# First layers of five blocks as seven products of half sums, second layers as one product at the end

## The chip, the cores and the metric

The kernel runs on one core of a Trainium2 chip. The metric is device time in microseconds (us): 341.78 us, the median of three runs (341.9, 341.78 and 339.52). The engines of the core are named as in the profile: PE (TensorE, matmul), DVE (VectorE), ACT (ScalarE), POOL (GpSimd) and SP (SyncE, which issues nearly all the DMAs here). They run side by side and wait for each other on semaphores.

## The reference

`x` is (2, 512, 1024), the context is (2, 1024, 1024). Both batches together are 1024 tokens of width 1024.

```python
def fake_quant(x, s, z):
    return (clip(round(x / s + z), 0, 255) - z) * s

x = x + tanh(g_xattn[0]) * matmul(fake_quant(layernorm(x)), fake_quant(ctx))

xt = layernorm(x).reshape(1024, 1024)
scores = softmax(xt @ router_w + router_b) + router_bias       # 16 experts
# 2 of 4 groups of experts, then 2 experts of those groups; gate = their scores
def step(y, p):
    w1, b1, w2, b2, w3, b3, ge = p
    h = silu(xt @ w1 + b1) * (xt @ w2 + b2)                    # 1024 -> 256
    return y + ge[:, None] * (h @ w3 + b3)                     # 256 -> 1024
y = scan(step, 0, all 16 experts)
z = silu(xt @ sw1 + sb1) * (xt @ sw2 + sb2) @ sw3 + sb3         # 1024 -> 512 -> 1024
x = x + tanh(g_ffn[0]) * (y + z)
```

With the inputs at hand all tokens choose the same two experts, so that two of the sixteen do work.

## The kernel before

**Precision.** The quantised product is exact in bf16. Every other large product is made to fp32 accuracy by splitting each operand into a high and a low part (`hi` is the operand cast to fp32r by ACT, `lo` the rest, a subtraction on DVE), and by three matmul passes: high times high, high times low, low times high. `split` (L308) does both steps for one operand.

**Tiling.** The tokens are 8 tiles of 128 (`NT`), 4 in each of the two batches; the contraction of 1024 is 8 slices of 128 (`KD`). A first-layer *block* is 128 hidden columns of `w1` and `w2` for all tokens: 4 shared ones (`SC`) and 2 for each expert (`EC`). For one block and one batch, `up_mm` (L327) accumulates w1's and w2's results in two PSUM banks with 2 x 3 x 8 matmuls of 128x512 (L335), so that a block is 96 matmuls. `up_post` (L341) applies bias, SiLU and gate product (L345 on ACT, L346 on DVE) and splits the hidden layer into its two parts. The second layer (`down`, L374) takes 128 tokens and accumulates all blocks of the shared network, or of one expert, in two PSUM banks; DVE then adds it, times the gate, onto the residual `X[t]` in SBUF (L386). A tile of the shared network takes 24 matmuls, one of an expert 12. Biases of the second layer are added by DVE from a broadcast row (`add_bias`, L393).

**Order.** The first part, up to 94.7 us, is a list written out by hand (`START`, L50, run under `manual_schedule`): layernorm, quantisation, attention product, second layernorm, transposes into `XH` and `XL` (the split activations with the contraction on partitions), and the first batch of shared columns 0 to 2 (steps `um`, `us`, `ug`, with `uh` and `ul` splitting the hidden). A step name is followed by its arguments: `mm.3.5` is the attention product of tile 3, slice 5. After this list the order is that of the code, and a planner puts it onto the engines' queues: shared column 0 for batch 1 (two halves), the router's input of batch 0 (`router_x`, L558: POOL adds `XH` and `XL` in four pieces, L563), shared column 1, the router's product (`router_logits`, L570), column 2, the router's product of batch 1, column 3 for both batches with the expert selection between (`choose` L607, a chain of small DVE operations, `count` L641 with one matmul, `next_expert` L652 twice, whose index is read into a register of SP at L673). Then `shared_down` (L704) for all 8 tiles, expert 0 (two blocks, then 8 tiles of second layer), expert 1. Weights come by SP's queue: `load_up` (L316) brings w1 and w2 of one block, 512 KB each; `load_down` (L353) a 128-row piece of `w3`. An expert's loads need its index.

**Buffers.** 22 `slabs` of 4 KB per partition hold raw and split weights and hidden parts in turn; `X` stays in SBUF for the whole run (8 tiles in `keep`), and so do `XH` and `XL`. A load into a slab waits until the slab's last user is through.

**End.** The last tile's second layer (`down_last`, L361) goes in columns of 512, 256 and 256. Two dynamic branches follow: one (L784, L785) repeats everything in a slower exact form if the quantisation's zero points don't fit; the other (L802 to L804) loops over further experts, if more than two were chosen. Neither is taken.

## Time and profile before

| | |
|---|---|
| median of the runs | 341.78 us |
| profiled execution | 340.19 us |
| its span in the trace | 338.5 us |
| first matmul after the hand-ordered list | 94.70 us |
| PE busy from there to 329.4 us | 234.69 of 234.70 us |
| one 128x512 matmul in an expert's first layer (43.52 us / 192) | 0.2267 us |
| last DVE operation ends | 329.9 us |
| DVE, 128x1024, two SBUF inputs (e0a0l, L312) | 1.22 us |
| ACT, cast of 128x1024 (e0a0h, L310) | 1.05 us |

The profiled execution's own time is 1.7 us longer than the span, and 1.6 us below the median of the runs. A row of the page's groups gives line, engine, operation, output and inputs with their sizes, how many there were, busy time in us and mean ns of one, and the idle time of the engine ahead of them with what ended it. Where the output of a whole block is meant, `e0p` stands for the first-layer banks of expert 0, `sp` for those of the shared network, `spo` and `e0po` for second-layer banks.

Four groups of the page, for their sizes and durations:

```profile
L241 PE MATMUL at<-cq,qT 128*128 128x512 bf16 x128 | 30.2, 379 | 2.4 <-POOL cq L161 1.4
L386 DVE SCALAR_TENSOR_TENSOR X<-spo,tg,X 128x512 f32<-128x512 f32 x16 | 11.3, 746 | 15.9 <-PE spo L383 15.9
L345 ACT ACTIVATE e0sa<-e0p,bv 128x512 f32<-128x512 f32 x4 | 2.8, 692 | 48.6 <-PE e0p L335 48.6
L394 DVE SCALAR_TENSOR_TENSOR X<-sbias,tg,X 128x1024 f32<-128x1024 f32 x8 | 10.3, 1285 | 0.3
```

DVE's and ACT's idle time in these rows is ended by PE: they have nothing to do until its matmuls are through.

### The profile page before, as it was taken

How to read it: one execution, taken by the hardware profiler on the slowest of the kernel's cores; microseconds unless marked ns; L12 is line 12 of the kernel's file. 1: busy time of each engine (PE TensorE's matmuls, PEld its weight loads, DVE VectorE, ACT ScalarE, POOL GpSimd, SP SyncE). 2: the span in 40 equal slices, each digit the busy share in tenths (PEclk: the TensorE clock that was granted, in tenths of full speed). 3: DMA queues.
4: the chain of work that ended last, by engine and by line, in shares of the span. 5: the costliest groups of instructions: out<-in, count | busy, mean ns of one | idle time of the engine just before them, and what ended most of it. 6: DMA issues, size and time to landing. Idle time of an engine off the chain costs nothing.

```text
span 338.5 us, 4322 instructions
## 1 busy us (share of the span) xinstructions
PE 318.1 (94%) x1673; PEld 254.7 (75%) x1673; DVE 197.0 (58%) x335; ACT 95.3 (28%) x148; POOL 78.6 (23%) x110
## 2 busy tenths in 40 slices
PE   6588899999999999999999999999999999999990
PEld 2244796769999776888888888888888888888870
DVE  3879999979812226845845441495385135944560
ACT  2657767873213135220200002211400012030000
POOL 2795798878600650000000000000000000000000
PEclk9799999999999999999999999999999999999996
DMA  6999940000004033100300092200410300001542
GB/s 190 420 375 381 409 106 0 2 0 2 0 2 124 3 126 124 64 0 25 99 2 0 0 293 81 63 2 12 112 62 2 124 0 2 0 0 61 191 185 75
DMA packets 25892, 31.45 MB, mean 93 GB/s; under 512 B 2492, under 2 KB 19204, under 8 KB 25860
## 3 DMA queue, kind: packets, MB, share of 16 engines
q1 hardware_dynamic: 25860, 31.05, 26.8%
q8 instruction: 17, 0.28, 0.3%
q14 instruction: 15, 0.12, 0.1%
HBM read 26.85 MB, written 4.19 MB: 92 GB/s over the span
## 4 chain that ended last, share of the span: by engine, by line
PE 75%; DVE 8%; POOL 5%; ACT 4%; issue 3%; DMA 2%; SPq 0%; DVEq 0%; POOLq 0%
PE sp L335 16%; PE e1p L335 13%; PE e0p L335 13%; PE sp L483 5%; PE spo L381 4%; PE spo L380 4%; PE spo L383 4%; ACT xn L262 2%; PE e0po L380 2%; PE e0po L383 2%; PE e0po L381 2%; PE e1po L380 2%; PE e1po L383 2%; PE e1po L381 2%; DMA X<-in_dram 2%
## 5 line engine op out<-in xcount | busy, mean ns | idle before, releaser
L241 PE MATMUL at<-cq,qT 128*128 128x512 bf16 x128 | 30.2, 379 | 2.4 <-POOL cq L161 1.4
L563 POOL TENSOR_TENSOR xf<-XH,XL 128x1024 f32<-128x1024 f32 x8 | 19.9, 2498 | 22.3 <-PE sp L335 19.5
L241 PEld LDWEIGHTS <-qT 128*128 128x128 bf16 x128 | 12.2, 98 | 15.4 <-issue 2.8
L386 DVE SCALAR_TENSOR_TENSOR X<-spo,tg,X 128x512 f32<-128x512 f32 x16 | 11.3, 746 | 15.9 <-PE spo L383 15.9
L346 DVE SCALAR_TENSOR_TENSOR ssa<-sp,bT,ssa 128x512 f32<-128x512 f32 (+1 forms) x6 | 4.0, 662 | 25.2 <-PE sp L335 25.2
L345 ACT ACTIVATE e0sa<-e0p,bv 128x512 f32<-128x512 f32 x4 | 2.8, 692 | 48.6 <-PE e0p L335 48.6
L386 DVE SCALAR_TENSOR_TENSOR X<-e0po,gv,X 128x512 f32<-128x512 f32 x16 | 11.3, 746 | 7.3 <-PE e0po L383 7.3
L386 DVE SCALAR_TENSOR_TENSOR X<-e1po,gv,X 128x512 f32<-128x512 f32 x14 | 9.9, 745 | 8.2 <-PE e1po L383 8.2
L291 DVE TENSOR_SCALAR xn<-X,nm,d 128x512 f32<-128x512 f32 x16 | 13.8, 890 | 1.0 <-POOL d L287 0.9
L345 ACT ACTIVATE e1sa<-e1p,bv 128x512 f32<-128x512 f32 x4 | 2.8, 689 | 34.1 <-PE e1p L335 34.1
L296 PE MATMUL px<-ident,xn 128*128 128x128 f32 x64 | 9.3, 275 | 3.0 <-DVE xn L291 1.9
L262 ACT ACTIVATE xn<-X,s 128x512 f32<-128x512 f32 x16 | 11.4, 716 | 1.9 <-DVE X L253 1.4
L173 DVE BATCH_NORM_STATS2 st<-X 128x6 f32<-128x512 f32 x16 | 10.3, 679 | 2.5 <-DMA X<-in_dram 2.5
L253 DVE SCALAR_TENSOR_TENSOR X<-at,cx_scale,X 128x512 f32<-128x512 f32 x16 | 11.6, 741 | 0.1
L346 DVE SCALAR_TENSOR_TENSOR e1sa<-e1p,bv,e1sa 128x512 f32<-128x512 f32 x4 | 3.0, 751 | 14.8 <-PE e1p L335 14.8
L296 PEld LDWEIGHTS px<-ident,xn 128*128 128x128 f32 x64 | 7.2, 141 | 5.0 <-ACT XH L153 2.2
L346 DVE SCALAR_TENSOR_TENSOR e0sa<-e0p,bv,e0sa 128x512 f32<-128x512 f32 x4 | 3.0, 750 | 13.5 <-PE e0p L335 13.5
L306 DVE TENSOR_TENSOR XL<-px,XH 128x512 fp32r<-128x512 f32 x16 | 10.4, 678 | 0.8 <-ACT XH L153 0.8
L394 DVE SCALAR_TENSOR_TENSOR X<-sbias,tg,X 128x1024 f32<-128x1024 f32 x8 | 10.3, 1285 | 0.3
L161 POOL TENSOR_SCALAR cq<-q8c,nz 128x1024 bf16<-128x1024 uint8 (+1 forms) x8 | 10.0, 1252 | 1.0 <-DVE q8c L231 0.6
L216 PE MATMUL pq<-ident_b,qx 128*128 128x128 bf16 x64 | 5.5, 231 | 4.6 <-ACT qx L159 4.3
L159 ACT ACTIVATE qx<-q8x,nz 128x1024 bf16<-128x1024 uint8 (+1 forms) x7 | 7.2, 1022 | 9.5 <-DVE q8x L205 9.5
(402 smaller groups left out, 830.0 us busy)
## 6 DMA issues: line engine op xcount, KB each, us to landing
cr<-in_dram SPq DMA_DIRECT2D x15, 512.0 KB, 9.9
out_dram<-X SPq DMA_DIRECT2D x15, 256.0 KB, 2.3
X<-in_dram SPq DMA_DIRECT2D x7, 512.0 KB, 9.2
X<-in_dram SPq DMA_DIRECT2D x2, 256.0 KB, 3.9
cr<-in_dram SPq DMA_DIRECT2D x2, 256.0 KB, 9.0
sb1r<-in_dram SPq DMA_DIRECT2D x1, 512.0 KB, 9.0
sa1r<-in_dram SPq DMA_DIRECT2D x1, 512.0 KB, 7.2
sb0r<-in_dram SPq DMA_DIRECT2D x1, 512.0 KB, 8.3
```

The costliest lines, as they stand in the source:

```text
L241: nc.tensor.matmul(acc[t][h], qT[b][:, t % TB, k, :], cq[b][:, k, half(h)], start=(k == 0), stop=(k == KD - 1))
L253: nc.vector.scalar_tensor_tensor(xs, acc[t][h], cx_scale, xs, ALU.mult, ALU.add, accum_out=sq_[t][0][:, h : h + 1])
L262: nc.scalar.activation(xn_[t][:, half(h)], X[t][:, half(h)], AF.Square, bias=s[:, h : h + 1], scale=-float(H), accum_out=q[:, h : h + 1],)
L291: nc.vector.tensor_scalar(xn_[t][:, half(h)], X[t][:, half(h)], nm, r, ALU.add, ALU.mult)
L296: nc.tensor.transpose(px_[t, q][:, k, :], xn_[t][:, ts(4 * q + k, P)], ident)
L335: nc.tensor.matmul(p, wx[:, k, :], xx[b][:, k, cols], start=first and k == 0, stop=last and k == KD - 1)
L380: nc.tensor.matmul(po[h], hh[:, ts(t, P)], wh[:, ts(h, 512)], start=first, stop=False)
L381: nc.tensor.matmul(po[h], hh[:, ts(t, P)], wl[:, ts(h, 512)], start=False, stop=False)
L383: nc.tensor.matmul(po[h], hl[:, ts(t, P)], wh[:, ts(h, 512)], start=False, stop=last)
L386: nc.vector.scalar_tensor_tensor(xs, po[h], scale, xs, ALU.mult, ALU.add)
L483: nc.tensor.matmul(up_[c, lo, i], w[:, k, :], x[0][:, k, lo : lo + 256], start=p == 0 and k == 0, stop=p == 2 and k == KD - 1,)
L563: nc.gpsimd.tensor_tensor(x, XH[b][:, ts(i, 2)].bitcast(F32), XL[b][:, ts(i, 2)].bitcast(F32), ALU.add)
```

## The change

Five blocks (shared column 3 and both blocks of both experts) no longer run as 96 matmuls but as seven products of 12. Tokens are halved by batch (index 1 and 2 of `A`), the contraction is halved (`KH` = 4 slices), and the two outputs, w1's and w2's, are the two column halves of `B`. This is Winograd's form of Strassen's scheme: sums S1 to S4 of activation halves are made once (from the router's unsplit inputs, in place), sums T1 to T4 of weight halves for every block, and the outputs are put together from seven products. All sums are split into high and low parts as other operands are.

Further: the hidden layer of every block and the residual pass through DRAM (`h_all`, `x_after`); the gate of an expert multiplies its hidden layer rather than its second layer's output, for which the gates of all tokens go to DRAM as one row and come back broadcast over the partitions; and the second layers of shared network and experts become one accumulation over all 8 blocks at the end, three tiles together first. The steps `uh` and `ul` leave the hand-ordered list, and `xd`, `ud`, `lv` (loads of w1 and w2 of shared column 2, taken out of `lw`) and `xx` come in. The pools become 16 slabs of 4 KB and 14 octs of 8 KB per partition, and `X` is in slabs. The two branches at the end become one.

```diff
-    slabs = ctx.enter_context(tc.tile_pool(name="slabs", bufs=22))
+    octs = ctx.enter_context(tc.tile_pool(name="octs", bufs=14))
+    slabs = ctx.enter_context(tc.tile_pool(name="slabs", bufs=NSLAB))
...
+    def xd(t):
+        nc.sync.dma_start(x_after[t], X[t])
+    def ud(c, lo):
+        nc.sync.dma_start(h_all[c][:, lo : lo + 256], sa_[c, lo])
...
+    def prep_pair(name, wa, wb):
...
+        split(wa, ah, al)
+        W["B11"], W["B21"] = (ah[:, lo], al[:, lo]), (ah[:, hi], al[:, hi])
...
+        sub = lambda out, p, q: nc.gpsimd.tensor_tensor(out, p, q, ALU.subtract)
+        sub(t13[:, lo], wb[:, lo], wa[:, lo])
+        sub(t24[:, lo], wb[:, hi], t13[:, lo])
+        sub(t13[:, hi], wb[:, hi], wb[:, lo])
+        sub(t24[:, hi], wa[:, hi], t24[:, lo])
+        for n, t in (("24", t24), ("13", t13)):
...
+            split(t, h, l)
...
+        W["B22"] = split(wb[:, hi], b22[:, lo], b22[:, hi])
+    def pair(name, W, b1, b2, ci, gates=None):
...
+        product(pa, "A11", "B11", True, False)
+        nc.scalar.copy(s1, pa)
+        product(pb, "S2", "T2", True, False)
+        nc.vector.scalar_tensor_tensor(s6, pb, b2, s1, ALU.add, ALU.add)
+        product(pa, "A12", "B21", False, True)
+        nc.scalar.activation(s11, pa, AF.Silu, bias=b1)
+        gated(s11, 0)
+        product(pb, "S3", "T3", False, False)
+        nc.vector.scalar_tensor_tensor(s7, pb, b2, s1, ALU.add, ALU.add)
+        product(pc, "S1", "T1", True, False)
+        product(pb, "A22", "T4", False, True)
+        nc.vector.tensor_tensor(s7, pc, s7, ALU.add)
+        nc.vector.tensor_tensor(s1, pb, s1, ALU.add)
+        nc.scalar.activation(s1, s1, AF.Silu, bias=b1)
+        gated(s1, 1)
+        product(pc, "S4", "B22", False, True)
+        done(s7, s1, 1)
+        nc.vector.tensor_tensor(s6, pc, s6, ALU.add)
+        done(s6, s11, 0)
...
+    wp = prep_pair("s3", *load_up("s", sw1c, sw2c, 3))
     sup(1, 1)
...
+    for i in range(2):
+        nc.vector.tensor_tensor(a22[i], a22[i], a21[i], ALU.add)
+    s1, s2, s3, s4 = a22, a11, a21, a12
+    for i in range(2):
+        nc.gpsimd.tensor_tensor(s3[i], a11[i], a21[i], ALU.subtract)
+    A["S2"] = sum_x("S2", s2, s1, a11, ALU.subtract, nc.vector)
+    for i in range(2):
+        nc.gpsimd.tensor_tensor(s4[i], a12[i], s2[i], ALU.subtract)
...
+    A["S3"] = split_x("S3", s3)
     sup(2, 1)
...
+    A["S1"] = split_x("S1", s1)
+    A["S4"] = split_x("S4", s4)
+    pair("s3", wp, sb1c(3), sb2c(3), 3)
...
+    for j, (e_, gv, bv) in enumerate(chosen):
+        nc.sync.dma_start(g_row[j].rearrange("(t p) -> p t", p=P), gv)
+        gates = slab(f"gates{j}", F32)
+        nc.sync.dma_start(gates, g_row[j].partition_broadcast(P))
+        for c in range(EC):
+            wp = prep_pair(f"e{j}_{c}", *load_up(f"e{j}", *expert_up(e_), c))
+            pair(f"e{j}_{c}", wp, bv[:, 0, c : c + 1], bv[:, 1, c : c + 1], SC + EC * j + c, gates)
...
+    for c in range(NC):
+        for n, src, got in (("h", h_all[c], hid), ("d", w3_rows(c), w3)):
+            raw = slab(f"{n}{c}r", F32)
+            nc.sync.dma_start(raw, src)
...
+    first, rest, last = (4, 5, 6), (7, 0, 1, 2), 3
...
-    zi = rt("zi", (P, 1), I32)
...
-    n_exp = nc.values_load(n_chosen[0:1, 0:1], min_val=2, max_val=E)
-    with tc.If(n_exp > 2):
-        with tc.For_i(2, n_exp):
-            expert(2, *next_expert(2), False)
```

The names that the prediction uses: in a block `x` (s3, e0_0, e0_1, e1_0, e1_1), `xs1`, `xs6` and `xs7` are the intermediate sums in SBUF, `t13` and `t24` the sums of weight halves (POOL, L378 of the changed kernel), `b22` the split lower half of w2; S3 and S4 are made on POOL at L739 and L742 of it. `done` stores the finished half of a hidden layer.

## The prediction

> **What bounds the kernel now.** I read four views. First the page's busy shares and its 40 slices:

> ```profile
> span 338.5 us, 4322 instructions
> PE 318.1 (94%) x1673; PEld 254.7 (75%) x1673; DVE 197.0 (58%) x335; ACT 95.3 (28%) x148; POOL 78.6 (23%) x110
> ...
> PE   6588899999999999999999999999999999999990
> ...
> PEclk9799999999999999999999999999999999999996
> ```

> From slice 11 on PE is full and at full clock, and POOL is idle after slice 15. Then the chain of waits in order of time:

> ```profile
> 94.86 22.43 PE sp L335 x144
> ...
> 198.76 43.52 PE e0p L335 x192
> 264.04 43.52 PE e1p L335 x192
> ```

> After the hand-ordered part the chain is PE alone. 43.52 us / 192 gives 0.2267 us for a 128x512 matmul. So a matmul removed there saves its full price, and any wait put in front of PE costs its full length, since nothing of PE is slack. Third, what feeds an expert. The timeline (start and length in us) of DVE's index and of SyncE's load issues:

> ```profile
> 157.26 0.14 DVE L657 TENSOR_SCALAR ei<-m 128x1 int32<-128x1 f32 x1
> ...
> 158.26 0.40 SPq L320 DMA_DIRECT2D e0a0r<-in_dram  x1
> 159.54 0.38 SPq L320 DMA_DIRECT2D e0b0r<-in_dram  x1
> ```

> Their landing (KB, us from issue) and the stretch up to expert 0's first matmul:

> ```profile
> e0a0r<-in_dram SPq DMA_DIRECT2D x1, 512.0 KB, 4.0
> e0b0r<-in_dram SPq DMA_DIRECT2D x1, 512.0 KB, 5.1
> ```

> ```profile
> 155.00:198.80 43.80, 43.80 (x196) 36.31 (x195) 26.06 (x49) 2.73 (x3) 0.00 (x0) 1.00 0.16 46
> ```

> Both weights of expert 0 had landed by 164.6 and PE took them up at 198.8. The last row (PE, PEld, DVE, ACT, POOL busy, clock, DMA share, GB/s) shows the shared second layer covering 34 us of loading and splitting. This cover is what the change removes. Fourth, rows that price POOL beside DVE: two of the timeline in the hand-ordered part and a group of the page (busy us, mean ns, idle before):

> ```profile
> 42.54 1.29 POOL L474 TENSOR_TENSOR sa0l<-sa0r,sa0h 128x512 fp32r<-128x512 f32 x1
> 42.60 1.24 DVE L190 TENSOR_TENSOR qa<-r,rs 128x1 f32<-128x1 f32 x1 [0.46 <-POOL r L186]
> L563 POOL TENSOR_TENSOR xf<-XH,XL 128x1024 f32<-128x1024 f32 x8 | 19.9, 2498 | 22.3 <-PE sp L335 19.5
> ```

> A DVE operation on one element per partition lasted 1.24 us, to the end of the POOL operation that had started just before it.

> [...] 4.29 us idle ahead of L216, and clock digit 7 in slice 2. [...] The change stores gate rows in 4-byte pieces; no row of before has such a store.

> **The change part by part**, against the profiled execution (340.2 us, of which the span is 338.5); the median of the runs, 341.8, is 1.6 higher. Prices without a line are the means of the same operation and size in before's groups: DVE 128x1024 with two SBUF inputs 1.22 (e0a0l), 128x512 0.68, a PSUM eviction 0.75; ACT's cast 1.05; POOL 128x512 1.28.

> *Matmuls.* Seven products of 12 matmuls take the place of 96: five blocks x 12 x 0.2267 = **-13.6 us**. Second layers keep 384 matmuls of 128x512 or their equal, so merging them saves PE nothing; 32 of 48 evictions (0.75 each) go, from a DVE that is 58% busy.

> *Hand-ordered part.* It loses the hidden splits (uh, ul) and gains stores of the residual and hidden on SP. The new waits: layernorm's buffer of tile 2 waits for the store of tile 0 (issued by about 40.5 here, needed at 53.8); the load of sa2r comes behind the store of tile 1 (lands about 49, needed 54.5). (Issue times are those of the same steps in before.) Both are hidden by attention's matmuls; if that cover is short, 2 us. I take **-0.5** (-2 to +2).

> *First Strassen block (shared column 3).* PE: both shared blocks and both router products are done by 120.8, sup(2,1) by 132.5, then the products at 2.72 each; the fourth (S3·T3) wants the second's bank evicted (s6) at 140.7. On DVE that eviction stands behind, all after the router's second product at 120.8 because the half sums overwrite the router's operands: 13 operations of 128x1024 (four sums, lo parts of t13, S1 to S4) at 1.22 = 15.9, b22 0.7, two evictions 1.5, some 20 small router operations 4.5. Total 22.6: 143.4, then 0.75 for itself, about 3 late. In the same stretch POOL does four 128x1024 subtractions for S3 and S4 at about 2.4. [...] 9.6 less what falls into DVE's waits, +7.5. s6 is then done near 151.3. Behind it: S3·T3 2.7, the s7 eviction 0.75, and the rest of the expert selection on DVE (some 20 x 0.22), on which PE's count matmul waits in the middle of the block; then A22·T4 and S4·B22, 5.4. The block ends near 162.5 instead of 151.5. I take **+10.5**; without lock +3, with twice its cost +14.

> *First expert block.* Before, the loads went out 1 us after the index. Now SP, in order, has ahead of them: the gate row's store (4-byte pieces), its broadcast reload that waits for it, and the two stores of the s3 hidden, the second of which waits for the last eviction of the s3 block. So the loads start after PE has run out of work, which is the change's largest wait: eviction and product 1.6, store issue and two loads 0.4 + 1.0 + 1.28 = 2.7 (the spacing of the rows above), landing 5.1, sharing with the gates' broadcast 1.0, four dependent POOL subtractions of 128x512 at 1.28 = 5.1, ACT's cast 1.05, handoffs 0.5. Together 17.1, less 2.7 for the first product, which needs only the w1 half: **+14.4** (13 to 18). The upper end is a slow gate row: the nearest row of before is the router weight's load in 64-byte pieces, 8.2 us beside other traffic; above some 4 us it holds the reload, and with it the expert's loads.

> *Second block of expert 0, then expert 1.* Within e0_0, 1.2. For e0_1: ACT's cast of the next block's t24 waits for four POOL subtractions on a late load and stands ahead of the PSUM copy e0_1s1, which the third product waits for: +4.5 (2.4 to 4.6). Sum **+5.7**. The next loads wait for buffers freed in time by the block before; I take 0 for e1_0 and e1_1 (0 to 3), hidden by 19 us of products each.

> *Reloads for the second layer.* h7's way through DRAM (about 2.3 out, 3 to 5 in, split 2) has some 15 us of other blocks' matmuls as cover, because tiles 4, 5, 6 run together block by block: 0 (0 to 3). Bias additions 3 x 1.28 per tile beside 10.9 us of matmuls: 0.

> *Clock.* Three gaps of 4.5 to 10 us should each return PE at half speed for 1 to 3 us: **+2** (0 to 5).

> *Tail.* One dynamic branch instead of two behind the last store; the second one's wait was 2.8 in before: **-2.5** (-4 to 0).

> Sum: -13.6 - 0.5 + 10.5 + 14.4 + 5.7 + 2 - 2.5 = +16.0: **356 us**.

> **Rivals.** (A) The sum above, 0.60. (B) Faster. The saving survives because the loads are not behind the s3 hidden's store: one mechanism, the place of the expert's loads in SP's queue. Were they out right after the index, as before, landing and POOL's work would lie beside the s3 block and the first product; the 14.4 and most of the 5.7 go. With the lock gone as well: 340.2 - 13.6 + 3 - 3 + 2 = 329. It decides if the loads go out 14 us ahead of the block's end. For it: 16 slabs might free early. Against it: the instruction order of SP in the changed program. 0.08, 324 to 336. (C) No lock and no cold clock: 356 - 7.5 - 2 - about 3 of the e0 waits, 343.5 (339 to 347), 0.14. Speaks for it: L563 shows 2.5 us each beside PE only. (D) The 4-byte store or the broadcast is slow, or PE comes back cold for longer: +4 to +10, 360 to 366, 0.18. Within D is a second layer that waits for spilled hidden, which needs more than 15 us per trip against 2.3 for a 256 KB store.

> **How the numbers follow.** The forecast is A's, 356. A's own range, from its bounds, 349 to 363; with C's and D's inner parts it reaches 341 to 366, leaving out B, a little of C below and D above. About 1% (338.4 to 345.2) is what a measurement of this kernel can tell from no change. Faster: B 0.08. Same: most of C, 0.12. Slower: A, D and C's top, 0.80.

> **What would show it.** Right: PE idle 11 us inside s3 ahead of S3·T3 and the count matmul, released by DVE; e0_0's T2 product behind a gap of about 14 us that ends in POOL's L378 or ACT's L325; e0a0r issued after s3s6's product; DVE 128x1024 lo parts near 2.4 beside POOL L739/L742; clock digits under 9 in those slices; PE's matmuls 60 fewer, nearly full from e1_1 on; one branch wait at the end. Wrong: e0a0r issued before 150 us; DVE's lo parts at 1.2 throughout; PE full through s3 and e0.

## The result, and the profile after

| | before | after |
|---|---|---|
| median of 4 runs each, us | 340.65 | 373.47 (372.97 to 373.68) |
| ratio, with its 95% interval | | 1.096 (1.091 to 1.101) |
| span of the profiled execution, us | 338.5 | 371.7 |

The change makes the kernel 32.8 us slower. The forecast was slower, 356, with a range of 341 to 366: the side was right, and the time lies 7 us beyond the range.

The first two parts of the page after, busy shares and the 40 slices:

```profile
span 371.7 us, 4423 instructions
...
PE 321.0 (86%) x1631; PEld 252.9 (68%) x1631; DVE 225.5 (61%) x344; ACT 112.7 (30%) x160; POOL 126.3 (34%) x138
...
PE   5697999986999997880279969999799998999994
...
PEclk9899999996999999697569989999989999999998
```

PE's row, full from slice 11 on before, now has an almost empty stretch at slices 19 and 20 (slices are counted from 1, as in the prediction). The clock row is the second thing to read: it is under 9 not only beside that hole but after each of the smaller ones. PE's busy time *rose*, 318.1 to 321.0, though its products need 13.6 us less: busy PE at half clock looks busy (from 271 to 272 us it is busy for 1.00 us at a granted clock of 0.50).

What PE waited for from 130 to 290 us (total, number, longest, in us):

```profile
PE e_0A L399 <- ACT e_0ah L325: 17.0, 1, 17.0
PE e_1A L399 <- ACT e_1s L414: 3.6, 1, 3.6
PE s3B L399 <- DVE S2l L326: 2.4, 1, 2.4
PE e_1B L399 <- DVE e_1s L421: 2.2, 1, 2.2
PE e_0B L399 <- ACT e_0t24h L325: 1.9, 1, 1.9
PE s3A L399 <- ACT s3s L414: 0.9, 1, 0.9
...
```

`e_0A` is bank A of a block of either expert, column 0; the wait of 17.0 is e0_0's, 3.6 that of e0_1. The releaser ACT is only the last link: its cast of e0a0r could start when that load had landed. Why it landed late is in SyncE's timeline (start, length):

```profile
164.43 1.96 SPq L761 DMA_DIRECT2D g_row<-gv  x2
174.74 0.33 SPq L763 DMA_DIRECT2D gates<-g_row  x1
175.16 0.86 SPq L410 DMA_DIRECT2D h_all<-s3s  x2
176.29 0.40 SPq L339 DMA_DIRECT2D e0a0r<-in_dram  x1
177.03 0.89 SPq L339 DMA_DIRECT2D e0b0r<-in_dram  x1
```

The queue stands for 10 us between the store of the gate row and its reload, although the last four matmuls of s3 had begun by 165.4. Then come the s3 hidden's stores and only then the expert's loads, 18 us later than in the kernel before.

PE's way through the five blocks, from the first product of s3 (139.49) to the first matmul of the second layer (276.96), one row a block (length; PE, PEld, DVE, ACT, POOL busy; clock; DMA share; GB/s):

```profile
139.40:166.40 27.00, 23.32 (x88) 17.38 (x86) 25.93 (x69) 11.43 (x14) 3.93 (x2) 0.87 0.05 10
166.40:208.80 42.40, 23.53 (x85) 18.63 (x85) 15.42 (x20) 9.54 (x12) 14.79 (x10) 0.76 0.37 111
208.80:233.40 24.60, 21.00 (x86) 16.86 (x85) 11.25 (x12) 5.98 (x8) 11.60 (x9) 0.93 0.21 66
233.40:253.80 20.40, 19.61 (x85) 15.61 (x84) 9.93 (x12) 5.79 (x7) 4.65 (x4) 1.00 0.30 104
253.80:276.96 23.16, 21.00 (x86) 16.85 (x85) 16.92 (x17) 13.93 (x16) 4.08 (x3) 0.93 0.72 273
```

A block's 84 products are worth 84 x 0.2267 = 19.0 us at full clock. Only e1_0, the fourth row, comes near that. In the others the length less the waits is still 2.0 to 4.5 us above 19.0, and the clock column says why.

The difference of the spans, 33.2, by the prediction's own terms:

| term | forecast | measured | from |
|---|---|---|---|
| hand-ordered part | -0.5 | +5.7 | first matmul after it: 94.70, then 100.35 |
| matmuls | -13.6 | -13.6 | 60 x 0.2267, counted, not timed |
| PE's waits in the five blocks | +30.6 | +29.0 | gaps in PE's timeline |
| clock in the five blocks | +2 | +13.3 | 137.47 - 5 x 19.04 - 29.0 |
| tail | -2.5 | -3.8 | last matmul to the end: 9.1, then 5.3 |
| second layer and the rest | 0 | +2.6 | what is left |

The clock term is a remainder, in which the few small matmuls of the expert selection are as well. By the trace's record of the granted clock, PE was at work for 21.4 us of this stretch at a clock of 0.50. Its matmuls of 128x512 start 0.43 us apart there (185.35 to 187.05), and 0.23 at full clock (274.19 to 275.12). So half of the 21.4, 10.7 of the 13.3, is my estimate of what was lost to the clock; the other 2.6 were not taken apart. **Two terms failed, the clock by 11 and the hand-ordered part by 6**; together they are the 17 us by which the forecast fell short.

### The profile page after: what moved, and what is told of

Same layout as the page of the kernel before. It is cut to its first block, busy times and chain, and to the rows that moved or that the text cites. A ratio compares the mean times of both kernels' runs of the same rounds, so it can differ in the third digit from the quotient of the medians.

```text
span 371.7 us, 4423 instructions
## 1 busy us (share of the span) xinstructions
PE 321.0 (86%) x1631; PEld 252.9 (68%) x1631; DVE 225.5 (61%) x344; ACT 112.7 (30%) x160; POOL 126.3 (34%) x138
## 5 line engine op out<-in xcount | busy, mean ns | idle before, releaser
L794 PE MATMUL po<-d,h 128*128 128x512 f32 (+1 forms) x119 | 44.9, 377 | 0.0
L793 PE MATMUL po<-d,h 128*128 128x512 f32 (+1 forms) x119 | 44.9, 377 | 0.0
L796 PE MATMUL po<-d,h 128*128 128x512 f32 (+1 forms) x119 | 36.9, 377 | 0.0
L818 DVE SCALAR_TENSOR_TENSOR Y<-po,tg,Y 128x512 f32<-128x512 f32 (+1 forms) x17 | 11.4, 713 | 29.7 <-PE po L796 29.7
L796 PEld LDWEIGHTS po<-d,h 128*128 128x128 f32 x119 | 22.4, 188 | 4.1
L793 PEld LDWEIGHTS po<-d,h 128*128 128x128 f32 x119 | 22.4, 188 | 4.1
L794 PEld LDWEIGHTS po<-d,h 128*128 128x128 f32 x119 | 22.4, 188 | 4.1
L597 POOL TENSOR_TENSOR xf<-XH,XL 128x1024 f32<-128x1024 f32 x8 | 19.1, 2417 | 12.8 <-DVE XL L315 12.8
L399 PE MATMUL e_0A<-XH,e_0ah 128*128 128x512 f32 x16 | 5.5, 479 | 17.0 <-ACT e_0ah L325 17.0
L814 DVE SCALAR_TENSOR_TENSOR Y<-eb,gt,Y 128x1024 f32<-128x1024 f32 x16 | 19.7, 1277 | 0.0
L305 PE MATMUL px<-ident,xn 128*128 128x128 f32 x64 | 10.9, 304 | 6.3 <-DVE XL L315 3.1
L399 PEld LDWEIGHTS e_0A<-XH,e_0ah 128*128 128x128 f32 x16 | 3.8, 242 | 18.2 <-ACT e_0ah L325 17.4
L378 POOL TENSOR_TENSOR e_0t<-e0b0r,e0a0r 128x512 f32<-128x512 f32 x1 | 1.9, 1855 | 39.5 <-DMA e0b0r<-in_dram 39.5
L524 PE MATMUL sp<-XH,sb 128*128 128x256 f32 x96 | 14.9, 303 | 0.0
L406 POOL TENSOR_TENSOR e_0s<-e_0s,gates 128x512 f32<-128x512 f32 x4 | 5.6, 1401 | 26.4 <-ACT e_0s L418 14.0
L524 PE MATMUL sp<-XH,sa 128*128 128x256 f32 x96 | 14.4, 297 | 0.0
L406 POOL TENSOR_TENSOR e_1s<-e_1s,gates 128x512 f32<-128x512 f32 x4 | 5.8, 1447 | 25.1 <-ACT e_1s L418 17.1
L814 DVE SCALAR_TENSOR_TENSOR Y<-sb,tg,Y 128x1024 f32<-128x1024 f32 x8 | 10.1, 1278 | 5.7 <-DMA Y<-x_after 5.7
## 6 DMA issues: line engine op xcount, KB each, us to landing
cr<-in_dram SPq DMA_DIRECT2D x15, 512.0 KB, 9.4
x_after<-X SPq DMA_DIRECT2D x8, 512.0 KB, 4.3
Y<-x_after SPq DMA_DIRECT2D x8, 512.0 KB, 11.6
X<-in_dram SPq DMA_DIRECT2D x7, 512.0 KB, 8.8
gates<-g_row SPq DMA_DIRECT2D x2, 512.0 KB, 4.2
```

Of the source, the lines that this page charges most:

```text
L305: nc.tensor.transpose(px_[t, q][:, k, :], xn_[t][:, ts(4 * q + k, P)], ident)
L399: nc.tensor.matmul(p, w[:, k, :], x[:, k, :], start=first and f and k == 0, stop=l and k == KH - 1, skip_group_check=not first,)
L406: nc.gpsimd.tensor_tensor(silu, silu, gates[:, ts(b, S)], ALU.mult)
L524: nc.tensor.matmul(up_[c, lo, i], w[:, k, :], x[0][k // KH][:, k % KH, lo : lo + 256], start=p == 0 and k == 0, stop=p == 2 and k == KD - 1,)
L597: nc.gpsimd.tensor_tensor(x, XH[b][i // 2][:, ts(i % 2, 2)].bitcast(F32), XL[b][i // 2][:, ts(i % 2, 2)].bitcast(F32), ALU.add)
L793: nc.tensor.matmul(p, hh[:, ts(t, P)], wh[:, cl], start=c == 0, stop=False)
```

## The experiments

My theory after the result, T1: the waits come from (a) the place of the loads in SyncE's queue, (b) POOL's sums beside DVE, and each wait is paid again in clock; the hand-ordered part is a displaced POOL operation. T2, the rival, differs from run to run and stands in the expectations. Runs with no interval are one execution each, beside a before of 340.57, or of 340.08 (rows_wdve, fixes_wdve, plain3_mixed). The four executions of after lie 0.7 us apart, but eleven of before up to 3.4 (339.23 to 342.65), so a difference of 4 to 5 us in one execution is read here together with the stage that moved.

### The gate row in pieces of 512 B (gate_rows)

```diff
-        nc.sync.dma_start(g_row[j].rearrange("(t p) -> p t", p=P), gv)
+        pgt = tbank(f"pgt{j}")[:NT, :P]
+        nc.tensor.transpose(pgt, gv, ident)
+        grow = rt(f"grow{j}", (NT, P))
+        nc.scalar.copy(grow, pgt)
+        nc.sync.dma_start(g_row[j].rearrange("(t p) -> t p", p=P), grow)
```

> The gate vector is transposed on PE and stored as 8 pieces of 512 bytes instead of 1024 pieces of 4 bytes; queue order unchanged. Theory 1 (piece size): in the changed kernel the store was issued at 164.4 us and the reload that waits for it only at 174.7, so the store takes 10 us and holds the expert's loads. With large pieces it lands in 2 to 3 us, the reload is then ahead of the s3 stores, the loads of e0a0r go out near 168.7 instead of 176.3, and the run is 7.5 us shorter: about 366 us. Theory 2 (order alone: the last eviction of s3 and the stores hold the queue, or the reload's own landing does): e0a0r moves by less than 2 us and the time stays at 372 to 374.

Measured 368.76, 4.7 less than after. SyncE's queue:

```profile
170.20 0.34 SPq L767 DMA_DIRECT2D gates<-g_row  x1
170.81 0.41 SPq L339 DMA_DIRECT2D e0a0r<-in_dram  x1
```

The load goes out 5.5 us earlier, and the wait on `e_0ah` falls from 17.0 to 9.6. But `e_0t24h` then costs 2.8 instead of 1.9, other waits 1 us more: sum of waits 23.6 instead of 29.0. The slow store was a part of the 17, not its whole.

### The hand-ordered part (router_in_list)

The step `router_x(0)`, POOL's sums of the router's operands, was left to the planner. Before, it put them behind the last two roots of the layernorm (POOL, then DVE's normalisations):

```profile
77.97 1.28 POOL L287 TENSOR_TENSOR d<-d,mhalf 128x1 f32<-128x1 f32 x2
...
79.81 5.10 POOL L563 TENSOR_TENSOR xf<-XH,XL 128x1024 f32<-128x1024 f32 x2
```

```profile
77.22 1.00 DVE L291 TENSOR_SCALAR xn<-X,nm,d 128x512 f32<-128x512 f32 x2
78.66 4.01 DVE L291 TENSOR_SCALAR xn<-X,nm,d 128x512 f32<-128x512 f32 x3 [0.45 <-POOL d L287]
```

After the change it put three of them ahead of these roots. POOL's timeline after, then DVE's:

```profile
73.70 7.27 POOL L597 TENSOR_TENSOR xf<-XH,XL 128x1024 f32<-128x1024 f32 x3
81.07 0.32 POOL L292 TENSOR_SCALAR d<-q,d 128x1 f32<-128x1 f32 x1
```

```profile
74.15 1.98 DVE L280 TENSOR_TENSOR d<-s 128x1 f32<-128x1 f32 x1
...
76.61 4.65 DVE L300 TENSOR_SCALAR xn<-X,nm,d 128x512 f32<-128x512 f32 x2
82.06 2.60 DVE L300 TENSOR_SCALAR xn<-X,nm,d 128x512 f32<-128x512 f32 x1 [0.79 <-POOL d L296]
```

Two things are to be seen: the roots `d` wait behind sums of 7.27 us, and DVE beside them takes 4.65 for two normalisations (1.00 in before, ahead of the sums), 1.98 for an operation on one element per partition. Before's row of 4.01 for three shows that the sums held DVE up there too, but there the roots were already done. The edit makes the sums the list's last step.

```diff
-ud.0.256
+ud.0.256 rx.0
...
-    xs = [router_x(0)]
```

> Only the four POOL sums of the router's input of batch 0 are put behind the last layernorm operation of the hand-ordered list. Theory 1 (POOL's order and its lock on DVE): three of these sums at 73.7 to 81.0 us stood ahead of two layernorm roots that DVE waited for, and DVE's own operations beside them took 4.65 us for two instead of 1.0. With them behind, the first matmul after the list moves from 100.35 back to about 95 and the run is 5 to 6 us shorter: about 368 us. Theory 2 (the added stores and buffers delay the list): first matmul after the list stays near 100, time 372 to 374.

Measured 368.92, 4.5 less; the first matmul after the list is at 95.03. The +5.7 is settled: 5.3 of it was the planner's order, and for stores and loads no more than 0.3 remains.

### S3 and S4 on DVE (sums_dve)

```diff
-        nc.gpsimd.tensor_tensor(s3[i], a11[i], a21[i], ALU.subtract)
+        nc.vector.tensor_tensor(s3[i], a11[i], a21[i], ALU.subtract)
...
-        nc.gpsimd.tensor_tensor(s4[i], a12[i], s2[i], ALU.subtract)
+        nc.vector.tensor_tensor(s4[i], a12[i], s2[i], ALU.subtract)
```

> The four subtractions of S3 and S4 (128x1024) are done by DVE instead of POOL. Theory 1 (lock): DVE operations beside them took 2.9, 3.2 and 3.4 us instead of 1.2, some 7.5 us in all, against 4 x 1.22 = 4.9 us of added work; the s6 eviction comes 2 to 3 us earlier and the run is 1 to 4 us shorter: about 371 us. Theory 2 (no lock, DVE bound by its number of operations): the s6 eviction comes 5 us later and the run is 4 to 5 us longer: about 378 us.

Measured 378.31, 4.8 *more* than after. By the total the rival wins (it had 378); by the stage it doesn't. DVE's operations beside POOL's S3 and S4 after, and the eviction s6, then the eviction in this run:

```profile
129.26 2.88 DVE L326 TENSOR_TENSOR s3t13l<-s3t,s3t13h 128x1024 fp32r<-128x1024 f32 x1 [0.34 <-issue]
...
134.33 3.21 DVE L728 TENSOR_TENSOR xf<-xf,xf 128x1024 f32<-128x1024 f32 x1
...
137.67 3.44 DVE L728 TENSOR_TENSOR xf<-xf,xf 128x1024 f32<-128x1024 f32 x1
...
142.71 1.93 DVE L651 TENSOR_TENSOR score<-ex,sm 128x128 f32<-128x128 f32 x1
...
154.60 0.74 DVE L416 SCALAR_TENSOR_TENSOR s3s<-s3B,bT,s3s 128x512 f32<-128x512 f32 x1
```

```profile
151.31 0.74 DVE L416 SCALAR_TENSOR_TENSOR s3s<-s3B,bT,s3s 128x512 f32<-128x512 f32 x1
```

In this run the four operations take 1.23, 1.22, 1.22 and 0.28, so DVE had lost 7.5 us beside POOL's sums. The prediction had put the same for what it calls the lock, DVE and POOL holding each other up as in its pair of rows at 42.5 us. In exchange DVE does four sums of about 1.2 more. Even so its eviction is done 3.3 us earlier, and the s3 block took 22.5 us (139.73 to 162.26) instead of 26.8: 4.3 is what this edit saves in the block, net of the added sums. What ate it is the queue:

```profile
190.38 2.07 PE L399 MATMUL e_0A<-XH,e_0ah 128*128 128x512 f32 x4 [28.12 <-ACT e_0ah L325]
```

The gate rows go out at 161.63 and 163.49, 2.5 to 2.8 us earlier, now with a store of the s3 hidden between them, but took up to 19.1 us to land. The first one's reload left at 173.67; e0a0r was issued at 174.72, hardly earlier, and landed 14.5 us after that. Why these transfers took longer than in after is open. So this run shows what DVE loses beside POOL in its stage and tells nothing of it by its total.

### The stores on another queue (rows_act), and three edits together (fixes)

rows_act is gate_rows with the s3 hidden's stores, the gate row and the gates on ACT's DMA queue, and with the last branch's condition made to depend on the last hidden, so that it is read late.

```diff
-            dq[0].dma_start(h_all[ci][:, ts(b, S)], h)
+            (nc.scalar if ci == 3 else dq[0]).dma_start(h_all[ci][:, ts(b, S)], h)
...
-        nc.sync.dma_start(gates, g_row[j].partition_broadcast(P))
+        nc.scalar.dma_start(gates, g_row[j].partition_broadcast(P))
```

> As gate_rows, and besides the two s3 hidden stores and the gate row's store and reload go to the queue of ACT, and the branch's condition is read late, so that SP asks for expert 0's weights right after both indices. Theory 1 (the order on SP is the rest of the e0_0 gap): e0a0r is issued near 166 instead of 168.7 in gate_rows, time 2 to 3 us below gate_rows, about 363.5 us; the index itself (163.4 in the changed kernel) is then what limits. Theory 2 (ACT's own order then holds the first cast, since its reload waits for the store): no gain over gate_rows, or a loss up to 3 us.

Measured 362.57, 6.2 less than gate_rows: e0a0r issued at 165.61 instead of 170.81. The other edits of the run weren't taken apart. fixes puts router_in_list and sums_dve on top.

> The four edits together (512-byte gate rows, s3 stores and gates on ACT's queue, branch condition read late, router sums behind the list, S3 and S4 on DVE), the order of the blocks unchanged. If their gains add: 373.5 - 10.9 - 4.5 - 3 = about 355 us, still some 14 us slower than before, because the expert's index comes only 3 us before the s3 block ends, so that landing (5), the sums of weights (5) and the cast (1) lie open on PE. Rival: the losses were one and the same wait seen four times (the late index), and the sum is 360 us or more.

Measured 354.67. The savings add up. Still, 18.9 us of waits are left, among them 4.7 on the load and 5.6 within the second block of expert 0, and 10.8 of clock and rest.

### The weight sums on DVE (rows_wdve, fixes_wdve)

`rows_wdve` is gate_rows, `fixes_wdve` is fixes, each with one word changed: the four dependent subtractions of T1 to T4 go from POOL to DVE.

```diff
-        sub = lambda out, p, q: nc.gpsimd.tensor_tensor(out, p, q, ALU.subtract)
+        sub = lambda out, p, q: nc.vector.tensor_tensor(out, p, q, ALU.subtract)
```

> gate_rows with the sums of weight halves on DVE instead of POOL, nothing else changed. Theory (POOL's sums are on the path of each expert block): four sums of 0.68 instead of 1.3 to 2.3 us; e0_0 begins its second product some 3 us earlier, and the 3.6 us wait of e0_1 on a PSUM copy that stands behind the t24 cast, with its cold clock, goes: 360 to 363 us against 368.8. Rival (they hide behind the landing of the next load): 367 to 369 us.

> The kernel fixes (354.7 us), with the sums of weight halves on DVE as well; s3 is still a Strassen block and the index is still late. Theory (two causes, POOL's sums and the lost cover): the waits of e0_1 and e1 shrink and the run is 8 to 10 us shorter, 344 to 347 us; the open landing ahead of e0_0 stays, some 14 us above plain3 (330.3). Rival (POOL's sums were nearly all of it): 336 us or less, and the order of the blocks matters little.

Measured 351.36 and 338.53: -17.4 and -16.1, about twice what I expected or more. 338.53 lies between my 344 to 347 and the rival's 336: POOL's sums weighed more than I gave them, but not nearly everything. The waits of gate_rows, then of rows_wdve, over the same stretch:

```profile
PE e_0A L399 <- ACT e_0ah L325: 9.6, 1, 9.6
PE e_1A L399 <- ACT e_1s L414: 3.6, 1, 3.6
PE e_0B L399 <- ACT e_0t24h L325: 2.8, 1, 2.8
...
PE e_1B L399 <- DVE e_1s L421: 2.4, 1, 2.4
```

```profile
PE e_0A L399 <- ACT e_0ah L325: 9.3, 1, 9.3
...
PE e_1B L399 <- DVE e_1s L421: 0.9, 1, 0.9
```

The wait on the load stays, the three behind POOL's sums go or shrink: ACT's cast of t24 no longer stands in its queue waiting for POOL, ahead of the copy that the third product needs. That is 8.0 us of waiting. The stretch shrank by 15.4. The rest is clock, as a comparison of the runs shows. The remainder is the length from the first product of s3 to the second layer, less 95.2, less waits; the last column is an estimate, half of the time that PE worked at a granted clock of 0.50, from the traces' record of the clock.

| run | waits, us | gaps over 1 us | remainder, us | lost at half clock, us |
|---|---|---|---|---|
| after | 29.0 | 2.4, 17.0, 1.9, 3.6, 2.2 | 13.3 | 10.7 |
| gate_rows | 23.6 | 2.4, 2.0, 9.6, 2.8, 3.6, 2.4 | 14.1 | 11.5 |
| rows_act | 22.9 | 2.5, 2.0, 7.2, 1.4, 5.9, 2.1 | 8.3 | 5.1 |
| fixes | 18.9 | 1.3, 1.1, 4.7, 2.3, 5.6, 2.2 | 10.8 | 8.2 |
| rows_wdve | 15.6 | 2.3, 1.6, 9.3 | 6.7 | 4.0 |
| fixes_wdve | 11.0 | 1.6, 1.1, 4.7, 2.2 | 3.8 | 1.5 |
| sums_dve | 39.4 | 1.3, 1.1, 28.1, 2.4, 4.2, 1.4 | 7.9 | 5.4 |

What the remainder holds besides the clock is 2.3 to 3.2 in every run, so it hardly depends on the waits. The loss at half clock follows the number of gaps, not their length: sums_dve waits longest and pays 5.4, gate_rows has most gaps and pays most. A gap that half clock follows costs 1.5 to 2.1 us in the mean of a run. No gap of 1.6 us or less is followed by it on its own, and not every gap of 2: those of 2.0 and 2.1 in rows_act and of 2.2 in fixes_wdve are not. The last section shows in what they differ.

### Loads, sums and gates put right, s3 as plain products (plain3)

If the causes are these, a version without them must keep the saving. plain3 runs shared column 3 plainly (96 products a block, so that four blocks save 48 x 0.2267 = 10.9 us), with the half sums made under its cover; selects the experts and issues the loads of e0 before that; takes all half sums and weight sums on DVE; and has the row in 512 B, the list and the late branch as above. Two smaller moves come with it: the reload of the gates goes behind the expert's first loads, and the split of S4 into the first expert block. So that the planner doesn't put the half sums ahead of the selection, they multiply by `one`, a number that is 1 and is known once both experts are.

```diff
-    wp = prep_pair("s3", *load_up("s", sw1c, sw2c, 3))
+    wsh[3] = [
...
+    one = rt("one", (P, 1))
+    nc.vector.tensor_scalar(one, chosen[1][1][:, 0:1], LOWEST, None, ALU.is_ge)
+    raws_up = load_up("e0", *expert_up(chosen[0][0]), 0)
+    sup(2, 1)
+    sup(3, 0)
+    sup(3, 1)
...
-        nc.vector.tensor_tensor(a22[i], a22[i], a21[i], ALU.add)
+        nc.vector.scalar_tensor_tensor(a22[i], a22[i], one, a21[i], ALU.mult, ALU.add)
...
-    pair("s3", wp, sb1c(3), sb2c(3), 3)
```

> Shared column 3 as a plain block of 96 matmuls per 1024 tokens again (2.7 us more for PE), and the expert selection first on DVE: the half sums S1 to S4 are made to wait for it, so that the weights of expert 0 are asked for ahead of shared columns 2 and 3, some 20 us before they are needed. Weight sums and S3, S4 on DVE, 512-byte gate rows, router sums behind the list, branch condition read late. Theory (lost cover): the saving of four blocks, 4 x 12 x 0.2267 = 10.9 us, shows once the expert's loads are covered: 340.2 - 10.9 - 3.8 (end) + 0.3 (list) + 1.5 (second layer) + 2 to 8 (remaining waits in the expert blocks) = 329 to 335 us, faster than before. Rival (the half sums and splits bind DVE, or slabs are too few, so that each expert block stalls by 5 us or more wherever the loads stand): 340 us or more.

One execution took 331.3 us. The same program over six executions:

> The same program as plain3, timed in five rounds against the kernel before: 331.3 us within 1 us, ratio to before 0.97 with an interval that excludes 1. If the single look was a lucky run: above 336.

330.29, ratio 0.972 (0.968 to 0.975): faster than before by 10.0 us, where the products alone give 10.9. From plain3_timed, SyncE's row of the load and PE's of the longest waits of the expert blocks (end of each row: idle before, releaser):

```profile
136.86 0.41 SPq L339 DMA_DIRECT2D e0a0r<-in_dram  x1
```

```profile
158.83 1.19 PE L399 MATMUL e_0A<-XH,e_0ah 128*128 128x512 f32 x4 [0.57 <-ACT e_0s L414]
166.28 1.20 PE L399 MATMUL e_0B<-S3h,e_0t13h 128*128 128x512 f32 x4 [0.58 <-DVE e_0s L416]
```

The load is out 39 us earlier than in after and lands under the plain block. No gap of the expert blocks is over 0.6 us, and from slice 4 on its page's clock digit is 9 throughout. Strassen's scheme itself was not the loss.

Three variants ask which part matters. **plain3_pool** puts only the weight sums back on POOL:

> plain3 with the sums of weight halves back on POOL. Theory [...]: POOL's four 128x512 operations per block take 1.3 to 2.3 us each beside a busy DVE [...]; the t24 parts come 3 to 6 us later per block, and waits of 1 to 4 us appear in e0_0 and e0_1: 333 to 340 us. Rival (POOL is free work): DVE loses 2.7 us of work per block and nothing waits longer: 330 to 332 us.

349.63, ratio 1.028 (1.024 to 1.033): 19 us lost by one word. POOL's timeline, DVE's beside it, and PE's:

```profile
147.66 9.12 POOL L378 TENSOR_TENSOR e_0t<-e0b0r,e0a0r 128x512 f32<-128x512 f32 x1 [46.62 <-PE sp L352]
158.95 1.26 POOL L378 TENSOR_TENSOR e_0t<-e0b0r,e_0t 128x512 f32<-128x512 f32 x1
```

```profile
149.88 2.35 DVE L326 TENSOR_TENSOR S3l<-xf,S3h 128x1024 fp32r<-128x1024 f32 x2
...
155.55 0.74 DVE L365 SCALAR_TENSOR_TENSOR sa<-sp,bT,sa 128x512 f32<-128x512 f32 x1
```

```profile
162.68 2.08 PE L399 MATMUL e_0B<-S2h,e_0t24h 128*128 128x512 f32 x4 [5.00 <-ACT e_0t24h L325]
```

The same subtraction takes 9.12 us beside DVE's row of two-input sums and 1.26 without. DVE isn't slowed (2.35 for two). My 333 to 340 had counted POOL's operations at 1.3 to 2.3 us each. Beside the wait of 5.00 PE has waits of 3.10, 1.56 and 5.35 in the expert blocks, and 6.5 us are lost at half clock. A part of this is something else: the planner also moved the second gates reload ahead of a load of expert 1 (issued at 211.6 instead of 190), and the wait of 5.35 comes after POOL has stood 12.19 us for that expert's last load. No run separates the two.

**plain3_bytes** puts the 4-byte store back:

> plain3 with the gate rows stored in 4-byte pieces again, as in the changed kernel. Theory (the store's 10 us cost only what waits for it): the stores are issued some 15 us before the reload is needed and behind expert 0's first loads, so the time stays at 331 us within 1.5. Rival (4-byte pieces stop whatever is behind them on the DMA engines, as the 14.5 us landing of e0a0r in sums_dve suggests): a store or load behind them lands some 10 us late and the run is 3 to 10 us longer than plain3.

329.86, ratio 0.971 (0.966 to 0.975), as plain3. The store still takes up to 11.8 us, but now the loads have gone out ahead of it. One of them, e0b0r, lands in 8.4 us instead of the 4.7 of plain3, which may be the store's doing, at no cost to PE here. What it cost in after is what stood behind it in the queue.

**plain3_mixed** leaves out the factor `one`, and the planner mixes half sums with the selection:

> plain3 without the tie that makes the half sums wait for the expert selection: the planner mixes both on DVE again, so that the index comes some 8 to 10 us later, near 146. Theory (the index must only be earlier than the cover's end by landing and preparation, about 12 us): shared column 3 ends near 155, so e0_0 waits 2 to 5 us: 332 to 336 us. Rival (the tie does nothing, plain3's gain is the block order alone): 329 to 331 us.

```profile
151.39 0.41 SPq L339 DMA_DIRECT2D e0a0r<-in_dram  x1
```

336.77, 5 to 6 us above plain3's runs: the load goes out 14 us later, and the longest wait of PE in the expert blocks is 2.05. That wait is followed by 3.4 us at half clock. Giving the selection DVE ahead of the half sums is a part of the saving.

## Why the prediction was right and wrong

**Right: the path.** The bound (PE without slack once the list is done), the saving of 13.6 (of the 10.9 of four blocks plain3 kept 10.0), and the main loss. e0a0r was issued at 176.29, after s3's end, behind the row's store, the reload and the s3 hidden's stores, as written. What DVE loses beside POOL's S3 and S4, 7.5 forecast and 7.5 measured, is right too; that all of POOL's time would be lost, less DVE's own waits, was an estimate for which before showed only the pair of rows at 42.5 us.

**Right in sum, shifted inside.** All waits together came to 29.0 for 30.6 forecast, and that closeness is in part luck. First Strassen block: +10.5 forecast, 3.6 of waits. The planner drew a part of S1·T1 forward, ahead of S3·T3, and the wait came at S2 instead. With 4.2 of clock and rest the block lost 7.8 of the 10.5. First expert block: 14.4 and 1.2 forecast, 17.0 and 1.9 waited. The row's store was priced as a rival ("above some 4 us it holds the reload") and not in the sum; it took 9.4. With 512-byte pieces (gate_rows) the same two waits are 9.6 and 2.8, so the sum's own sizes were 3 us too high, and the store that it left out made up for that. Second block of expert 0: 4.5 forecast, 3.6; the queueing on ACT that it named is what rows_wdve took away. For e1_0 and e1_1 I took 0 (0 to 3); 0.8 and 2.2.

**Wrong: "Clock. Three gaps of 4.5 to 10 us should each return PE at half speed for 1 to 3 us: +2 (0 to 5)."** Measured 13.3, of which 10.7 by the estimate from the record of the clock. Each of its figures was short: five waits, not three; a wait of 1.9 to 2.2 was enough; and PE worked at half clock for 3.4 to 6.0 us after each. The size came from the one place of before's trace with a gap of 4.29 us, where the clock digit was 7 in one slice; a slice of 8.5 us is too coarse to show how long a half clock lasts. The same trace's record of the clock has 0.50 there from 11.5 to 14.9, 3.4 us. Rival D had PE at half clock for longer, at 0.18 and with 366 as its top.

**Wrong: "Hand-ordered part ... I take -0.5 (-2 to +2)."** Measured +5.7. I looked for waits on stores and buffers in what the diff adds to the list. The loss came from something that the diff doesn't touch: a POOL step with no fixed place, which the planner moved. The pair of rows with which the prediction priced the lock is from this very part of the kernel, and I used the price only for S3 and S4.

**Short: what hangs on POOL's weight sums.** Their length was nearly right: the four of e0_0 took 5.65 us for 5.1 forecast. Taking them from POOL gave 16 to 17, about half of it through the clock, where the forecast had 5.7 of small waits and no clock behind them. Rivals B and C fall as they were written: B had the place of the loads right (in plain3 they go out early and it pays), but early loads with POOL's sums (plain3_pool) are still slower than before; C had neither DVE's loss beside POOL nor the clock, and both are there (7.5 us and, by the estimate, 10.7).

## What to carry to other kernels

Where PE is the bound, price a new wait as its length plus what the trace shows at half clock behind it (here an estimated 1.5 to 2.1 us for each wait that it followed), and count waits of 2 us too, though some of these went free here (2.16 us in fixes_wdve). A saving in PE's work is worth its price only if loads, sums and selection that feed the shorter work are moved earlier with it: look at what stands ahead of each load in its queue, and at what POOL and DVE do side by side (a subtraction of 1.26 us took 9.12 here). When a planner orders the work, read the new order of the steps that the diff doesn't touch as well.

## What the runs showed of the hardware that was not expected

**Half clock after short waits.** In before, outside the end, half clock followed one gap, of 4.29 us. In after a wait of 2.2 us was enough. Windows of 1 us in after (same columns as above), the wait ending at about 270:

```profile
268.00:269.00 1.00, 0.00 (x0) 0.00 (x0) 1.00 (x2) 0.80 (x2) 0.00 (x0) 1.00 1.01 414
271.00:272.00 1.00, 1.00 (x4) 0.81 (x3) 1.00 (x2) 0.88 (x1) 0.00 (x0) 0.50 1.02 410
274.00:275.00 1.00, 1.00 (x6) 0.82 (x5) 0.61 (x2) 0.00 (x0) 0.00 (x0) 1.00 0.00 0
```

PE stands still in the first with the clock at 1.00; the half clock comes when PE is already at work again (270.5), and goes at 274.0. Over the five waits of after it came 3.0 to 5.1 us after the gap began. Waits of 0.58 us and less left the clock at 1.00 (plain3_timed, 150 to 176 us).

**POOL and DVE side by side.** Which of the two is held up differs from place to place. In plain3_pool a POOL subtraction took 9.12 us beside DVE's back-to-back two-input operations, and 1.26 where DVE stood idle; DVE lost nothing (2.35 for two of 128x1024). The 9.12 ended 1.23 us after DVE had begun, at 155.55, an operation with one of its tensors in PSUM. In the list after the change DVE was held up: beside POOL's sums two normalisations took 4.65 us instead of 1.00, a one-element operation 1.98 instead of 0.16. In that place the normalisations have only one tensor input. Beside S3 and S4, DVE's two-input operations took 2.88 to 3.44 us instead of 1.22 to 1.23. What decides between these cases was not shown.

**4-byte pieces.** A row of 1024 values stored in 4-byte pieces took 9.4 us to land in after, up to 11.8 in plain3_bytes and up to 19.1 in sums_dve. As 8 pieces of 512 bytes its reload could go out 1.75 us after the stores' issue began (gate_rows). What sets the length wasn't taken apart.
